# A two-layer graph network on one core: six sums per batch move from GpSimd to VectorE, two copies change engine, and the loads, writes and sums of a few batches take other steps

## The chip, the cores and the metric

The kernel runs on one core of a Trainium2 chip. The metric is the device time of one execution in microseconds. A core has TensorE (matmuls), VectorE, ScalarE, GpSimd and SyncE; the profile calls them PE, DVE, ACT, POOL and SP. Each works through its own list of instructions in order, and semaphores let one wait for another. SyncE issues almost all DMAs here, GpSimd a few.

## The reference

All arithmetic is in float32. There are 32 batches of 512 nodes with 512 features; the adjacency matrices are 512 x 512 for each batch.

```python
# layer 0
h = relu(layernorm(x))
deg = sum(adj, axis=-1)
agg = (adj @ h) / max(deg, 1e-6)
x = x + relu(concat([h, agg]) @ W0.T)
# layer 1
h = relu(layernorm(x))
q, k = split(h @ Wqk); v = h @ Wv
agg = adj @ (k * mask)
w = (q * agg).sum(-1) * mask / sqrt(512)
x = x + softmax(w, over the nodes)[:, None] * v
```

## The kernel before

The kernel rearranges the algebra so that each batch needs four groups of products: Y (transposed h times the right half of W0), O (h times the left half plus scaled adj times Y, which gives the new x), TV (the new h times a combined weight matrix and Wv), and U (adj times masked h). Every product of 512 x 512 matrices is done with seven products of half-size blocks in place of eight, in the manner of Winograd and Strassen. That needs sums and differences of the blocks of each operand beforehand and of the results afterwards. Operands live in tiles of seven slots: four slots hold the blocks, three take sums.

`left_sums` and `right_sums` (lines 102 to 115) give the four additions of a left and of a right operand, in an order in which a later one uses an earlier one. `add` and `sub` (lines 93 to 97) do them on VectorE, or on the engine given as `on`. `copy` (line 100) is a ScalarE activation. `product` (from line 118, matmuls at line 130) is a generator: it issues the matmuls of one step and yields, and between them it issues the copies of a finished PSUM tile (`pp`, `pq`) and the additions of results (`pr`, `m5`, `pq`). It uses its seven blocks in the order 1, 2, 6, 5, 7, 3, 4. A TV step (matmuls at line 467) works in the same way on four PSUM banks.

The instruction order of every engine is written by hand. `Plan.at(n, f)` puts a piece of work behind step n of the running phase, and `run` plays a phase and its plan. So the place of a line in the plan fixes where its instructions stand on every engine, with the DMAs on SP among them. An engine that waits holds up everything behind it on its own list. O and TV have 14 steps, U and Y have 7. The main loop runs O(i), TV(i-1), U(i), Y(i+1) for i from 0 to 31; batch 0 has a start of its own in `start()`.

The work beside the products comes in these classes:

- `FrontH` (batch b, first h): `load` reads x in two halves into buffers of tag `n` (two buffers), `stats` takes statistics on VectorE, `variance` and `shift` finish them (a power on GpSimd at line 248 between two VectorE instructions), `write` normalizes on ScalarE (line 258) and sends the chunk to a DRAM scratch `dhT`, `to.read` brings it back to `shT` in another order and `turn` transposes it on VectorE into `hT` (tile `wide`).
- `FrontA` (adj): `load` into the same two `n` buffers, `sum` adds a row on ScalarE (line 330), `degrees` clamps and inverts on VectorE (lines 334 and 335), `write` scales on ScalarE (line 343) and sends to `daT`; `turn` fills the tile `aT`, and `sums` calls `left_sums` on it.
- `FrontH1` (second h): statistics, `write`, `mask` (line 379), `masked_sums`, `turn`, `sums` and `inner_sums` (tile `h1T`); `keep` stores the new x as `dx`.
- `Stream` loads the seven blocks of W0's left half again in every batch (`w<-dw`, line 409), three buffers.
- `Post` (the end of a batch, during the next batch's phases): `recombine` on tile `tv`, `dot`, softmax pieces, `apply` on ScalarE (line 566), `add_x1`, a GpSimd DMA that adds the stored x (line 573, `tv<-dx`), and `store` on SP (line 589), which waits for it.

In O the plan before gives the four sums of Y and two of the four sums of adj to GpSimd:

```python
right_y = right_sums(of(Y[i]), nc.gpsimd)
p.at(1 + k // 2, FA[i].sums, k, nc.gpsimd)
```

Of the kernel before, what the change touches and what calls it, by code (L numbers as in the profile page):

```python
# [22 lines left out]
def kernel(  # L23
# [35 lines left out]
    nc = tc.nc  # L59
    B, N, F = x.shape  # L60
    C = N // P
# [37 lines left out]
    def copy(o, i):  # L99
        nc.scalar.activation(o, i, AF.Copy)  # L100

    def left_sums(s, on=None):

        return [
            lambda: add(s(4), s(2), s(3), on), lambda: sub(s(6), s(0), s(2), on),
            lambda: sub(s(5), s(4), s(0), on), lambda: sub(s(2), s(1), s(5), on),
        ]

    def right_sums(s, on=None):
        return [  # L110
            lambda: sub(s(4), s(1), s(0), on), lambda: sub(s(6), s(3), s(1), on),
            lambda: sub(s(5), s(3), s(4), on), lambda: sub(s(1), s(2), s(5), on),
        ]

    def of(t):
        return lambda i: t[:, i]
# [104 lines left out]
    X, AT_, DEG, W, Y, H1M, H1T, U, TV = ({} for _ in range(9))  # L221
# [65 lines left out]
    class FrontH:  # L287
# [23 lines left out]
        def sums(self, i):  # L311
            left_sums(of(hT))[i]()

    class FrontA:
# [33 lines left out]
                AT_[self.b] = slots("aT", 1, f"aT_{self.b}")  # L348
            self.to.turn(h, AT_[self.b])

        def sums(self, i, on=None):
            left_sums(of(AT_[self.b]), on)[i]()

    class FrontH1:

# [278 lines left out]
        for k in range(C):  # L634
            nc.tensor.transpose(p[:, ts(k, P)], src[:, ts(k, P)], identity)

    def keep_chunk(dst, c, name):
        copy(
            dst[:, 2 * (c // 2):2 * (c // 2) + 2, :, ts(c % 2, P)],
            held.pop((name, c)).rearrange("p (a b i) -> p a b i", a=2, b=2),  # L640
        )

    FH, FA, F1 = {}, {}, {}
# [25 lines left out]
    def start():  # L669
# [3 lines left out]
        fa = FA[0] = FrontA(0)  # L673
# [9 lines left out]
        fh = FH[1] = FrontH(1)  # L683
# [17 lines left out]
        h0 = hT  # L701
# [3 lines left out]
        for c in range(C):  # L705
            v = block(f"h_{c}").rearrange("p a f -> p (a f)")
            nc.scalar.activation(
                in_order(v), natural(X[0][:, c, :]), AF.Relu, scale=t[1][:, c:c + 1], bias=t[2][:, c:c + 1]
            )
            turn_chunk(v, c, "h")  # L710
            if c > 0:
                keep_chunk(h0, c - 1, "h")
        keep_chunk(h0, 3, "h")
        r2, l0 = right_sums(of(w2R)), left_sums(of(h0))
        for f in r2[:3] + l0[:3] + r2[3:] + l0[3:]:
            f()
# [12 lines left out]
        p = Plan()  # L729
# [23 lines left out]
        p = Plan()  # L753
# [47 lines left out]
        p = Plan()  # L801
# [47 lines left out]
    with tc.manual_schedule(engines=engines):  # L849
        weights, mvR = start()  # L850
        post = None
        for i in range(B):
# [4 lines left out]
            if i > 0:  # L857

                p = Plan()
                for n in range(4):  # L860
                    p.at(2 * n + 1, stream.load)
                right_y = right_sums(of(Y[i]), nc.gpsimd)
                p.at(0, right_y[0])
                p.at(0, right_y[2])
                for k in (1, 3):
                    p.at(1 + k // 2, FA[i].sums, k, nc.gpsimd)
                    p.at(1 + k // 2, right_y[k])
                if i == 1:
                    for k, g in enumerate(weights[4:]):
                        p.at(3 + 2 * k, g)  # L870
                    fa = FA[2]
                    for h in range(2):
                        for c in range(2):
                            p.at(2 + 2 * h + c, fa.sum, 2 * h + c)
                            p.at(6 + 2 * h + c, fa.write, 2 * h + c)
                        p.at(4 + 2 * h, fa.degrees, h)
                    FH[3] = FrontH(3)
                    p.at(10, FH[3].load, 0)
                    p.at(11, FH[3].load, 1)
                f1 = F1[i - 1]  # L880
                for k in range(4):
                    p.at(k // 2, f1.sums, k)
                if post is not None:
                    for c in range(C):
                        p.at(2 + c, post.apply, c)
                    p.at(3, post.add_x1, 0)
                    p.at(5, post.add_x1, 1)
                    p.at(9, post.store, 0)
                    p.at(11, post.store, 1)
                for k in range(4):  # L890
                    p.at(2 + k, f1.inner_sums, k, 0, 7)
                if 1 < i and i + 2 < B:
                    fh = FH[i + 2]
                    for c in range(C):
                        p.at(3 + c, fh.stats, c)
                        p.at(10 + c, fh.write, c)
                    p.at(7, variance, fh.t)
                    p.at(9, shift, fh.t)
                if more:
                    th = FH[i + 1]  # L900
                    p.at(2, th.to.read, 1)
                    p.at(11, th.turn, 0)
                if 1 < i and i + 2 < B:
                    fa = FA[i + 2] = FrontA(i + 2)
                    p.at(12, fa.load, 0)
                p.at(12, f.stats, 0)
                p.at(12, f.stats, 1)
                p.at(13, variance, f.t, 0, 2)
                run(layer0_out(i, stream.take), 14, p)


                post = Post(i - 1, F1[i - 1])
                p = Plan()
                p.at(0, f.stats, 2)
                p.at(0, shift, f.t, 0, 2)
                p.at(0, f.stats, 3)
                p.at(1, variance, f.t, 2, 4)
                if last:
                    p.at(1, FA[i].factor)
                p.at(3, shift, f.t, 2, 4)  # L920
                for c in range(C):
                    p.at([2, 3, 5, 6][c], f.write, c)
                    p.at(8 + c, f.mask, c)
                p.at(1, f.keep)
                for k in range(4):
                    p.at([10, 12, 12, 12][k], f.masked_sums, k)
                if 1 < i and i + 2 < B:
                    p.at(1, fa.load, 1)
                    for h in range(2):
                        for c in range(2):  # L930
                            p.at(4 + 2 * h + c, fa.sum, 2 * h + c)
                        p.at(7 + 2 * h, fa.degrees, h)
                if i == 1:
                    fa = FA[3] = FrontA(3)
                    p.at(11, fa.load, 0)
                    p.at(13, fa.load, 1)
                    fh = FH[3]
                    for c in range(C):
                        p.at(4 + c, fh.stats, c)
                        p.at(9 + c, fh.write, c)  # L940
                    p.at(7, variance, fh.t)
                    p[9].insert(0, lambda t=fh.t: shift(t))
                if more:
                    p.at(3, th.turn, 1)
                    for k in range(4):
                        p.at(5 + k // 2, th.sums, k)
                p.at(8, f.to.read, 0)
                p.at(9, f.to.read, 1)
                for k in range(7):
                    p.at(12 + k // 4, post.recombine, k, 0, 0)  # L950
                run(layer1_tv(i - 1), 14, p)


            p = Plan()
# [7 lines left out]
            if i == 0:  # L962
                fh = FH[2]
# [35 lines left out]
            if more:  # L999
                p = Plan()  # L1000
                fb = FA[i + 1]
                p.at(2, fb.turn, 0)
                p.at(3, fb.turn, 1)
                p.at(4, fb.sums, 0)
                p.at(4, fb.sums, 2)
                p.at(1, load_x, i + 1)
                if i + 2 < B:
                    p.at(5, FH[i + 2].to.read, 0)
                if i > 0:
                    p.at(0, post.shift)  # L1010
                    p.at(1, post.exponents)
                    p.at(2, post.row_sum)
                    p.at(4, post.weights)
                    for k in range(7):
                        p.at(3 + k // 2, post.recombine, k, None, 1)
                p.at(2, FA[i].factor)
                if i == 0:
                    for c in range(C):
                        p.at(c, fh.write, c)
                    for k in range(1, 4):  # L1020
                        p.at(3 + k, weights[k])
                    FA[2] = FrontA(2)
                    p.at(3, FA[2].load, 0)
                    p.at(6, FA[2].load, 1)
                elif i == 1:
                    p.at(0, fa.degrees, 1)
                    for c in range(C):
                        p.at(2 + c, fa.write, c)
                    FH[4] = FrontH(4)
                    p.at(5, FH[4].load, 0)  # L1030
                    p.at(6, FH[4].load, 1)
                elif i + 3 < B:
                    p.at(0, FH[i + 3].load, 1)
                run(layer0_y(i + 1), 7, p)

        final = Post(B - 1, F1[B - 1])
        p = Plan()
# [71 lines left out]
```

## Time and profile before

| | |
|---|---|
| median of 4 runs | 2297.28 us (2296.23 to 2299.43) |
| the profiled execution's own time | 2296.23 us |
| its span in the profile | 2294.1 us |
| PE busy | 2248.9 us (98%) |
| DVE busy | 1968.2 us (86%) |
| ACT busy | 1027.9 us (45%) |
| POOL busy | 508.6 us (22%) |
| DMA moved | 463.65 MB, 202 GB/s |

The busy time of an engine is the sum over its instructions in one profiled execution; register, branch, semaphore and DMA-issuing instructions are not counted. The own time holds about 2 us outside the span. The profile names a group of instructions by line, engine, operation and tiles (`out<-in`, buffer numbers left out); a wait is named by the waiting instruction and by what released it. The phases of the middle batches follow each other evenly: O takes 24.2 us, TV 21.15, U and Y 12.1 each.

### The profile page before, as it was taken

What the parts mean: (1) busy time and instruction counts of PE and PEld (TensorE: products, weight loads), DVE (VectorE), ACT (ScalarE), POOL (GpSimd) and SP (SyncE); (2) the same over time, 40 slices, a digit from 0 to 9 for tenths busy, and PEclk for the clock granted to TensorE, in tenths of its full rate; (3) what the DMA queues carried; (4) which work ended last, traced back from release to release, by engine and by line L of the source; (5) the groups of instructions that cost most, each with busy time, mean ns of one, the idle gap of its engine ahead of it and who ended that gap; (6) DMA issues with size and microseconds to landing.
All of it is one profiled execution on the core that took longest, in us unless ns stands there. A gap on an engine that the chain in (4) does not pass through costs nothing.

```text
span 2294.1 us, 32535 instructions
## 1 busy us (share of the span) xinstructions
PE 2248.9 (98%) x10372; PEld 1968.5 (86%) x10372; DVE 1968.2 (86%) x3619; ACT 1027.9 (45%) x1903; POOL 508.6 (22%) x453
## 2 busy tenths in 40 slices
PE   7999999999999999999999999999999999999996
PEld 6788888888888888888888888888888888888885
DVE  6798898888898888898888988888988889888878
ACT  4454434444444544344454344443444543444332
POOL 0202222112222112222022221122220222211222
PEclk9999999999999999999999999999999999999998
DMA  9978877877778877777877778877778787787552
GB/s 220 226 202 229 214 195 194 223 216 210 207 191 205 226 218 205 207 183 211 229 215 207 194 185 228 218 201 202 193 205 226 215 207 199 191 219 213 152 139 64
DMA packets 409594, 463.65 MB, mean 202 GB/s; under 512 B 37680, under 2 KB 271152, under 8 KB 405328
## 3 DMA queue, kind: packets, MB, share of 16 engines
q1 hardware_dynamic: 400176, 428.56, 69.1%
q0 software_dynamic: 8928, 32.51, 8.0%
q8 instruction: 82, 1.34, 0.3%
q14 instruction: 88, 0.72, 0.1%
q10 hardware_dynamic: 320, 0.52, 0.1%
HBM read 293.93 MB, written 167.51 MB: 201 GB/s over the span
## 4 chain that ended last, share of the span: by engine, by line
PE 82%; DVE 8%; DMA 5%; SPq 2%; issue 1%; POOL 1%; ACT 1%; DVEq 0%; ACTq 0%; POOLq 0%
PE ptv L467 23%; PE pp_o L130 16%; PE pp_y L130 9%; PE pp_u L130 8%; PE pq_o L130 8%; PE pq_y L130 4%; PE pq_u L130 4%; PE pr_o L130 4%; PE pr_y L130 2%; PE pr_u L130 2%; DVE tv L94 2%; DMA dhT<-n 2%; DMA tv<-dx 1%; DMA a<-in_adj_dram 1%; SPq L204 1%
## 5 line engine op out<-in xcount | busy, mean ns | idle before, releaser
L467 PE MATMUL ptv<-mv,h1T 128*128 128x256 f32 x3136 | 684.3, 379 | 6.2 <-ACT m_tv L100 4.8
L467 PEld LDWEIGHTS ptv<-mv,h1T 128*128 128x128 f32 x3136 | 595.0, 190 | 90.3 <-ACT m_tv L100 7.6
L94 DVE TENSOR_TENSOR tv<-tv 128x256 f32<-128x256 f32 (+1 forms) x644 | 322.0, 512 | 11.6
L97 DVE TENSOR_TENSOR h1T<-h1T 128x512 f32<-128x512 f32 (+2 forms) x195 | 277.7, 1437 | 1.2
L100 ACT ACTIVATE tv<-ptv 128x512 f32<-128x512 f32 (+1 forms) x372 | 188.0, 540 | 151.0 <-PE ptv L467 144.8
L130 PE MATMUL pp_y<-wide 128*128 128x256 f32 x1024 | 243.5, 381 | 2.5 <-ACT y L100 2.5
L130 PE MATMUL pp_o<-y,aT 128*128 128x256 f32 x1024 | 241.9, 379 | 0.0
L130 PE MATMUL pp_u<-h1m,aT 128*128 128x256 f32 x1024 | 241.9, 379 | 0.0
L130 PE MATMUL pp_o<-w,wide 128*128 128x256 f32 x992 | 234.4, 379 | 0.5 <-ACT o L100 0.5
L130 PEld LDWEIGHTS pp_y<-wide 128*128 128x128 f32 x1024 | 195.5, 191 | 29.6 <-ACT y L100 2.9
L97 POOL TENSOR_TENSOR y<-y 128x512 f32<-128x512 f32 x124 | 216.2, 1743 | 15.5 <-DVE y L94 12.9
L130 PEld LDWEIGHTS pp_u<-h1m,aT 128*128 128x128 f32 x1024 | 194.6, 190 | 26.9 <-issue 0.5
L130 PEld LDWEIGHTS pp_o<-y,aT 128*128 128x128 f32 x1024 | 194.5, 190 | 26.4
L548 POOL PARTITION_ALL_REDUCE gtop<-top x32 | 12.5, 391 | 903.4 <-DVE top L545 885.5
L130 PEld LDWEIGHTS pp_o<-w,wide 128*128 128x128 f32 x992 | 188.4, 190 | 26.5 <-ACT o L100 0.9
L100 ACT ACTIVATE o<-pp_o 128x512 f32<-128x512 f32 x96 | 57.3, 597 | 298.3 <-PE pp_o L130 298.3
L100 ACT ACTIVATE y<-pp_y 128x512 f32<-128x512 f32 x128 | 76.4, 597 | 239.1 <-PE pp_y L130 234.1
L248 POOL TENSOR_TENSOR rstd<-rstd,mhalf 128x2 f32<-128x2 f32 (+1 forms) x96 | 78.4, 817 | 446.2 <-DVE rstd L247 446.2
L100 ACT ACTIVATE xu<-pp_u 128x512 f32<-128x512 f32 x128 | 76.4, 597 | 198.0 <-PE pp_u L130 198.0
L94 DVE TENSOR_TENSOR tv<-ptv,m_tv 128x512 f32<-128x512 f32 (+1 forms) x124 | 73.1, 622 | 103.3 <-ACT m_tv L100 89.8
L94 DVE TENSOR_TENSOR tv<-ptv,tv 128x512 f32<-128x512 f32 x248 | 141.7, 613 | 13.9 <-PE ptv L467 11.2
L330 ACT ACTIVATE a<-a 128x512 f32<-128x512 f32 x128 | 80.2, 627 | 110.1 <-DMA a<-in_adj_dram 110.1
(113 smaller groups left out, 3465.7 us busy)
## 6 DMA issues: line engine op xcount, KB each, us to landing
w<-dw SPq DMA_DIRECT2D x217, 256.0 KB, 3.2
xu<-in_x_dram SPq DMA_DIRECT2D x128, 256.0 KB, 5.3
a<-in_adj_dram SPq DMA_DIRECT2D x256, 128.0 KB, 3.1
dh1T<-h1m SPq DMA_DIRECT2D x128, 256.0 KB, 3.3
dx<-xu SPq DMA_DIRECT2D x32, 1024.0 KB, 5.0
sh1T<-dh1T SPq DMA_DIRECT2D x256, 128.0 KB, 3.3
shT<-dhT SPq DMA_DIRECT2D x248, 128.0 KB, 4.7
daT<-a SPq DMA_DIRECT2D x124, 256.0 KB, 3.0
```

Of the source, the lines that this page charges most:

```text
L94: (on or nc.vector).tensor_tensor(o, a, b, op=ALU.add)
L97: (on or nc.vector).tensor_tensor(o, a, b, op=ALU.subtract)
L100: nc.scalar.activation(o, i, AF.Copy)
L130: nc.tensor.matmul(p[:, rc, :], lt[:, LEFT[k], dk, ts(rc, P)], right[:, dk, :], start=first and n == 0, stop=True, skip_group_check=True,)
L204: nc.sync.dma_start(out=t[q * R:(q + 1) * R, :, :], in_=rows[:, 2 * h:2 * h + 2, :])
L248: nc.gpsimd.tensor_tensor(rstd[:, a:b], rstd[:, a:b], mhalf[:, a:b], op=ALU.pow)
L330: nc.scalar.activation(v, v, AF.Copy, accum_out=DEG[self.b][:, c:c + 1])
L467: nc.tensor.matmul(banks[n][:, :, ts(i, P)], left[:, LEFT[k], LEFT_IN[j], :], mvR[:, RIGHT[k], RIGHT[j], :, :], start=first and i == 0, st ...
L548: nc.gpsimd.partition_all_reduce(self.gtop, self.top, channels=P, reduce_op=ReduceOp.max)
```

## The change

Seven edits, in three phases of the main loop and in the start:

1. The four sums of Y in O go to VectorE, and so do the two sums of adj; sums 1 and 3 of both stand at steps 2 and 4, where they stood at 1 and 2. `FrontA.sums` loses its engine argument.
2. In the start, the four normalizations of batch 0's h and their transposes are issued first, and then the four copies out of PSUM; the first two of these copies go to VectorE.
3. Y of batch 1: the four writes of h of batch 2 stand at steps 2, 3, 4 and 4 (before: 0 to 3), and the first load of adj of batch 2 at step 5 (before: 3). On SP the four x loads of batch 1 now stand ahead of these writes, and the reads `shT` ahead of both adj loads.
4. O of batch 1: the writes of adj of batch 2 stand at steps 8 to 11 (before: 6 to 9), the degrees at 5 and 7 (before: 4 and 6).
5. O of batch 1: the loads of x of batch 3 stand at steps 12 and 13 (before: 10 and 11).
6. TV from batch 2 of the loop on: the sums over adj stand at steps 4, 6, 8 and 10 (before: 4 to 7).
7. There, too, the degrees stand at 8 and 12 (before: 7 and 9).

```diff
-        def sums(self, i, on=None):
-            left_sums(of(AT_[self.b]), on)[i]()
+        def sums(self, i):
+            left_sums(of(AT_[self.b]))[i]()
...
-    def keep_chunk(dst, c, name):
-        copy(
+    def keep_chunk(dst, c, name, by=copy):
+        by(
...
             turn_chunk(v, c, "h")
-            if c > 0:
-                keep_chunk(h0, c - 1, "h")
-        keep_chunk(h0, 3, "h")
+        for c in range(C):
+            keep_chunk(h0, c, "h", nc.vector.tensor_copy if c < 2 else copy)
...
-                right_y = right_sums(of(Y[i]), nc.gpsimd)
+                right_y = right_sums(of(Y[i]))
                 p.at(0, right_y[0])
                 p.at(0, right_y[2])
                 for k in (1, 3):
-                    p.at(1 + k // 2, FA[i].sums, k, nc.gpsimd)
-                    p.at(1 + k // 2, right_y[k])
+                    p.at(2 + 2 * (k // 2), FA[i].sums, k)
+                    p.at(2 + 2 * (k // 2), right_y[k])
...
                             p.at(2 + 2 * h + c, fa.sum, 2 * h + c)
-                            p.at(6 + 2 * h + c, fa.write, 2 * h + c)
-                        p.at(4 + 2 * h, fa.degrees, h)
+                            p.at(8 + 2 * h + c, fa.write, 2 * h + c)
+                        p.at(5 + 2 * h, fa.degrees, h)
                     FH[3] = FrontH(3)
-                    p.at(10, FH[3].load, 0)
-                    p.at(11, FH[3].load, 1)
+                    p.at(12, FH[3].load, 0)
+                    p.at(13, FH[3].load, 1)
...
-                            p.at(4 + 2 * h + c, fa.sum, 2 * h + c)
-                        p.at(7 + 2 * h, fa.degrees, h)
+                            p.at(4 + 4 * h + 2 * c, fa.sum, 2 * h + c)
+                        p.at(8 + 4 * h, fa.degrees, h)
...
                     for c in range(C):
-                        p.at(c, fh.write, c)
+                        p.at([2, 3, 4, 4][c], fh.write, c)
...
                     FA[2] = FrontA(2)
-                    p.at(3, FA[2].load, 0)
+                    p.at(5, FA[2].load, 0)
                     p.at(6, FA[2].load, 1)
```

## The prediction

> **What bounds the kernel now.** I read the page first, then TensorE's own waits, then the timelines of one batch in the middle, and last the places where TensorE stands still.
>
> ```profile
> span 2294.1 us, 32535 instructions
> PE 2248.9 (98%) x10372; PEld 1968.5 (86%) x10372; DVE 1968.2 (86%) x3619; ACT 1027.9 (45%) x1903; POOL 508.6 (22%) x453
> ```
>
> TensorE is the bound: 2248.9 of 2294.1 us. In the batch from 449.78 to 519.28 it never stops, so a batch costs 69.5 us whatever the others do. A change of order and engine can only win what TensorE waits, and lose by making it wait. Its waits (total us, times, longest):
>
> ```profile
> PE h L635 <- ACT h L707: 14.1, 2, 13.6
> PE ptv L467 <- ACT m_tv L100: 4.8, 6, 2.0
> PE pp_y L130 <- ACT y L100: 2.5, 1, 2.5
> PE pq_o L130 <- DMA w<-dw: 1.5, 1, 1.5
> PE ptv L467 <- DVE h1T L97: 1.2, 1, 1.2
> PE pp_o L130 <- ACT o L100: 0.5, 1, 0.5
> ```
>
> Outside the first 13.6 us, about 11 us can be had. The timelines of O in that middle batch show how VectorE and GpSimd stand there (start, us, engine, line):
>
> ```profile
> 451.79 1.75 DVE L94 TENSOR_TENSOR h1T<-h1T 128x512 f32<-128x512 f32 x1
> 453.47 5.12 DVE L97 TENSOR_TENSOR h1T<-h1T 128x512 f32<-128x512 f32 x3
> 458.62 2.04 DVE L94 TENSOR_TENSOR h1T<-h1T 128x896 f32<-128x896 f32 x1
> 460.58 2.15 DVE L97 TENSOR_TENSOR h1T<-h1T 128x896 f32<-128x896 f32 x1
> 464.78 1.08 DVE L97 TENSOR_TENSOR h1T<-h1T 128x896 f32<-128x896 f32 x1
> ...
> 476.46 0.68 DVE L442 SCALAR_TENSOR_TENSOR xu<-pp_o,xu 128x512 f32<-128x512 f32 x1
> 451.44 3.23 POOL L97 TENSOR_TENSOR y<-y 128x512 f32<-128x512 f32 x2 [0.21 <-DVE y L94]
> 461.73 1.97 POOL L573 DMA_DIRECT2D tv<-dx  x2
> ```
>
> While GpSimd does the six sums (451.44 to 461.7) a 128x896 add takes VectorE 2.04 to 2.15 us, and 1.08 once they are over. A 128x512 add takes 1.71 there, 0.69 elsewhere (the aT and wide groups). Only after its sums can GpSimd issue tv<-dx, and the output stores on SP wait for that (243.6 us in SP's waits). The costliest of the six m_tv waits, in the batch from about 1565:
>
> ```profile
> 1587.92 2.20 SPq L589 DMA_DIRECT2D out_dram<-tv  x4
> 1594.88 1.74 SPq L204 DMA_DIRECT2D a<-in_adj_dram  x4
> 1599.03 0.63 ACT L330 ACTIVATE a<-a 128x512 f32<-128x512 f32 x1 [5.01 <-DMA a<-in_adj_dram]
> 1604.78 0.63 ACT L330 ACTIVATE a<-a 128x512 f32<-128x512 f32 x1 [1.29 <-DMA a<-in_adj_dram]
> 1605.41 1.06 ACT L100 ACTIVATE m_tv<-ptv 128x512 f32<-128x512 f32 x2
> 1606.04 6.31 PE L467 MATMUL ptv<-mv,h1T 128*128 128x256 f32 x28 [1.97 <-ACT m_tv L100]
> ```
>
> Late store, late write of h behind it, late load of adj into the same buffers, ScalarE stuck on a sum over adj with the m_tv copies queued behind: TensorE loses 1.97 us. The wait in Y of batch 1 has the same form:
>
> ```profile
> 88.71 0.16 DVE L252 SCALAR_TENSOR_TENSOR nmr<-mv,rstd 128x4 f32<-128x4 f32 x1 [0.62 <-POOL rstd L248]
> 88.91 0.81 ACT L258 ACTIVATE n<-n,nmr,rstd 128x512 f32<-128x512 f32 x1 [4.00 <-DVE nmr L252]
> 89.63 0.58 ACT L100 ACTIVATE y<-pp_y 128x512 f32<-128x512 f32 x1
> 90.26 1.99 PE L130 MATMUL pp_y<-wide 128*128 128x256 f32 x8 [2.53 <-ACT y L100]
> ```
>
> **Part 1, sums of Y and adj on VectorE (31 batches).** Added to VectorE: 186 adds of 128x512 at 0.69 us, 128 us, or 0.605 start to start, 3.6 us a batch. Given back: 96 h1T adds at 1.373 instead of 0.69 (66 us), 93 at 1.545 and 31 at 2.048 instead of 1.08 (43 and 30), 32 at 0.920 (7): 146 us. VectorE's busy time falls by some 18 us, to about 1950. Its order in O, from 451.8: two sums of y to 453.1, four h1T adds to 455.5, aT and y to 456.7, two 896 adds to 458.7, statistics to 459.5, o and xu to 460.8, aT and y to 462.0, then as before. TensorE's steps begin every 1.727 us from 449.78. It needs y's slot 5 at step 5 (458.4; ready 453.1), slots 6 at step 9 (465.3; 456.7), aT's slot 2 at step 11 (468.8; 461.4), y's slot 1 at step 13 (472.2; 462.0). Nothing is within 5 us, so the sums cost the path nothing, under TensorE's 24.2 us of O; uncovered, they would be 3.6 us a batch. VectorE reaches shift (470.66 today) about 2.5 us sooner. GpSimd issues tv<-dx when ScalarE's apply is done, near 455.4 and 456.6 instead of 461.7. Its landing took 5.6 to 8.9 us, so the stores at steps 9 and 11 find it done; the writes of h and the eight loads of adj behind them on SP come 2.5 us sooner, and by up to 5 in the bad batches.
>
> A rule against this: the Trainium skill, "SBUF — State Buffer", under "SBUF: two separate sides", says that VectorE can lock GpSimd out of their shared port so that it can't write the descriptors of its own DMAs, and gives 3100 ns for a DMA of 620. VectorE's adds would now stand around tv<-dx. The row: issued at 461.73 beside a two-input add of VectorE, it took 1.97 us for two; over all 62, 0.87 to 1.20 each. By the row it moves 5 us forward; by the rule each loses 2.5 and both moves are eaten, and the adj loads stay late (case B). I take the row, since the same kind of add was beside it.
>
> **Part 2, sums over adj at every second step of TV.** The adds stay at four of 0.63 + 0.19 us; on ScalarE the third and fourth now stand behind the m_tv copies, with a mask between. Behind a late load wait only masks, which VectorE's h1m adds and U need at the end of TV; in my count the masks end 17.2 us into TV, against 19.1 in the middle batch. The second half of adj (used at 487.6, 13.6 into TV) has about 3 us in hand. VectorE's second degrees come after the h1m adds, and the writes of adj in U find them. Of the m_tv waits (0.40, 0.81, 0.20, 0.93, 1.97, 0.45: 4.76) a late first half could leave some; bounds 3.0 and 4.76, and as parts 1 and 2 both help, I take 4.3.
>
> **Part 3, h of batch 2 written later in Y of batch 1.** The copy of y now precedes the first write, so the 2.53 us go. Next on ScalarE is the second y copy, behind one write: 88.9 + 0.7, then ready at 90.2, needed at 91.0. Slack 0.8 us, so the next wait is not far. On SP the four x loads come forward, the four dhT writes stay, and the four shT reads go ahead of the eight adj loads: issue at about 96 and 98, against 97.7 and 102.3. The w load behind them lands near 104.5, needed at 106.8. Bounds 1.7 to 2.53, take 2.5.
>
> **Part 4, adj of batch 2 written later in O.** The copies m_o and o now precede the writes that wait for VectorE's degrees: the 0.48 us go. VectorE starts y's sums near 98.9 and ends the last mv add near 118.6 (122.4 today); TensorE needs it at 121.5. L442 frees a PSUM bank near 125.0, needed at 125.9. The x loads of batch 3 (eight DMAs) stay behind the four daT writes; they land near 124 and 127, before their statistics. Take 0.5.
>
> **Part 5, the first copies.** ScalarE's four normalizations run without copies between, so the transposes wait neither the 0.53 us at 16.09 nor the 0.1 before 17.27. VectorE pays two PSUM copies, not in the trace as such; its adds out of PSUM take 0.68, and it sits idle 2.08 us at 19.05: nothing. But TensorE runs here at half pace (eight matmuls of pp_y in 3.42 us from 18.18, then 0.216 each from 21.4; the page's PEclk row is too coarse to show it). By the row alone, full pace came 5.3 us after the gapless start at 16.09; that start moves to 13.59, worth 1.5 us. The Trainium skill, "TensorE: Matmul & The Clock Gate", "What's actually happening", has windows of 3.4 us that run free of the program: either the same window (0.3 us, half the gap) or the one before (2.0). I take 1.2, range 0.3 to 2.0. All that follows up to batch 1 is paced by TensorE (through its pm products at 65.3) and moves along.
>
> Left: the w wait at 181.4 (adj, then x loads ahead of it on SP) and h1T at 2254, whose cover does not change: 0.
>
> **Sum.** 1.2 + 2.5 + 0.5 + 4.3 = 8.5 us off the profiled execution's 2296.23 (span 2294.1): 2287.7. That run was the fastest of four; the median is 1.05 higher, so 2288.8.
>
> **Rivals.** B: tv<-dx is held up, or VectorE's lead is lost in waits for statistics, and the m_tv waits stay: 4.2 us, 2293.1. For: the port rule; against: part 2 alone takes two sums out of the way. D: the early waits only move to the next place (0.8 us of slack in Y, 0.9 at L442, the w loads): 4.3 to 5 us, 2292.8. For: an ordering this tight at 70 us; against: everything there was counted.
> C, slower: VectorE becomes the bound in O. If the long h1T adds do not shrink, 3.6 us come on top. L442 ends at 477.14 and frees a bank that the second product of TV needs at 478.7 to 479.1. From about 1.8 us of added VectorE time TensorE waits every batch: (3.6 - 1.8) x 31 = 56 us, 2353. Against it: the same add takes 1.08 at 464.78 and 2.15 at 460.58, in one batch.
>
> **How the numbers follow.** Two kernels closer than 0.2% (4.6 us) can't be told apart. Forecast 0.68 (2285 to 2291.5), B 0.15, D 0.10, C 0.07. B and D lie on the border of 2292.7: half of them count as faster. Faster 0.68 + 0.12 = 0.80, same 0.13, slower 0.07. The range runs from 2285.0 (all waits gone, early clock) to 2294.5, over B and D.
>
> **What would show it.** Right: 128x512 h1T adds near 0.69 us and 896 near 1.08, VectorE near 1950 us; tv<-dx issued before the seventh step of O; no wait on y near 88, none on m_tv; TensorE still at 69.5 us a batch. Wrong: a wait on VectorE at L467 in every batch (C), tv<-dx taking 3 us on GpSimd (B), a new wait at 90 to 130 (D).

## The result and the profile after

The changed kernel takes 2292.44 us (median of 31 runs, 2289.2 to 2297.14), the kernel before beside it 2296.62 us (51 runs). The ratio is 0.9982, 95% interval 0.9977 to 0.9987: 4.2 us less. A second comparison gave 0.9990 (0.9983 to 0.9996). Both intervals stay below 1, and the gain is under the 0.2% that the prediction called measurable. The prediction said 8.5 us and 2288.8. The time lies outside the band given to the forecast itself (2285 to 2291.5) and inside the full range of 2285.0 to 2294.5, which was drawn over rivals B and D as well. About half of the forecast gain is missing, and the profile shows a new loss at one place.

The page of the changed kernel, its own time 2293.06 us:

```profile
span 2291.0 us, 32519 instructions
PE 2248.0 (98%) x10372; PEld 1970.3 (86%) x10372; DVE 1931.1 (84%) x3807; ACT 1027.8 (45%) x1901; POOL 183.8 (8%) x267
```

VectorE has taken on 186 additions and yet is busy for 37 us less; GpSimd keeps a third of its time. TensorE's waits (total us, times, longest):

```profile
PE h L635 <- ACT h L707: 13.5, 1, 13.5
PE pq_o L130 <- DMA w<-dw: 7.6, 1, 7.6
PE ptv L467 <- DVE h1T L97: 1.2, 1, 1.2
PE ptv L467 <- DVE xu L94: 0.2, 1, 0.2
```

The waits on y, o and m_tv are gone, all the waits that the sum counted on. The wait for w has grown from 1.5 to 7.6 us. TensorE's timeline there, in O of batch 2 (start, duration, and in brackets the idle time before and what ended it):

```profile
172.62 1.89 PE L130 MATMUL pp_o<-y,aT 128*128 128x256 f32 x8
182.12 3.75 PE L130 MATMUL pq_o<-w,wide 128*128 128x256 f32 x8 [7.61 <-DMA w<-dw]
185.66 2.15 PE L130 MATMUL pq_o<-y,aT 128*128 128x256 f32 x8
187.65 1.89 PE L130 MATMUL pp_o<-w,wide 128*128 128x256 f32 x8
```

The same wait in the kernel before:

```profile
181.41 1.97 PE L130 MATMUL pq_o<-w,wide 128*128 128x256 f32 x8 [1.47 <-DMA w<-dw]
```

After the wait of 7.61 us the next eight matmuls take 3.75 us where eight take 1.89, and the eight after those 2.15: TensorE comes back at half clock, about half its full pace. The granted clock shows it, 0.74 and 0.58 of full speed in two windows of 5 us (the columns: busy time of PE, PEld, DVE, ACT and POOL, then granted PEclk, DMA share, GB/s). After:

```profile
177.00:182.00 5.00, 0.00 (x0) 0.00 (x0) 4.93 (x8) 0.00 (x0) 0.00 (x0) 0.74 1.04 214
182.00:187.00 5.00, 4.88 (x13) 4.00 (x14) 3.77 (x9) 0.00 (x0) 0.94 (x1) 0.58 0.96 203
```

Before:

```profile
177.00:182.00 5.00, 3.53 (x17) 2.82 (x16) 4.93 (x4) 0.60 (x1) 5.00 (x4) 1.00 0.98 223
```

The DMA engines are near full load in both kernels (share 1.04 and 0.98), so the share alone does not explain the late w. What differs is which transfers are in flight beside it, and this stands in the timelines of SP and GpSimd. After:

```profile
167.89 5.37 SPq L204 DMA_DIRECT2D n<-in_x_dram  x8
173.36 0.37 SPq L409 DMA_DIRECT2D w<-dw  x1
171.95 2.10 POOL L573 DMA_DIRECT2D tv<-dx  x2 [3.54 <-ACT tv L566]
```

Before:

```profile
171.52 5.37 SPq L204 DMA_DIRECT2D n<-in_x_dram  x8
176.99 0.37 SPq L409 DMA_DIRECT2D w<-dw  x1
184.24 2.09 POOL L573 DMA_DIRECT2D tv<-dx  x2
```

The w load is issued 3.6 us earlier than before, but lands 8.6 us after its issue. The two accumulating stores tv<-dx of batch 0, 512 KB each, are issued 12.3 us earlier, mostly because GpSimd has no sums ahead of them (9.3 us in e3_sums_alone below), and now stand 1.4 us ahead of w. The DMA view of 160 to 192 us (issues, KB each, median us to landing), after:

```profile
tv<-dx POOLq DMA_DIRECT2D x2, 512.0 KB, 8.7
w<-dw SPq DMA_DIRECT2D x4, 256.0 KB, 8.4
```

and before:

```profile
w<-dw SPq DMA_DIRECT2D x4, 256.0 KB, 4.6
tv<-dx POOLq DMA_DIRECT2D x2, 512.0 KB, 7.2
```

Three numbers account for the two profiles. "Arrival" is when TensorE is free for the `pq_o` product that waits for w (start of the product before it, plus 1.73); "next block" is the start of pp_o after the two pq_o products; "rest" is the span less that.

| profile | arrival | w wait | next block | rest | span |
|---|---|---|---|---|---|
| before | 179.78 | 1.47 | 184.94 | 2109.2 | 2294.1 |
| changed | 174.35 | 7.61 | 187.65 | 2103.4 | 2291.0 |

TensorE arrives 5.4 us earlier; from arrival to the next block it takes 13.3 us instead of 5.2 (6.1 more of waiting, 2.0 at half clock); the rest, free of m_tv waits, is 5.8 us shorter. 5.4 - 8.1 + 5.8 = 3.1 us, the difference of the two spans.

### The profile page after: what moved, and what is told of

It is laid out like the page before. It is cut to its first block, busy times and chain, and to the rows that moved or that the text cites. A ratio compares the mean times of both kernels' runs of the same rounds, so it can differ in the third digit from the quotient of the medians.

```text
span 2291.0 us, 32519 instructions
## 1 busy us (share of the span) xinstructions
PE 2248.0 (98%) x10372; PEld 1970.3 (86%) x10372; DVE 1931.1 (84%) x3807; ACT 1027.8 (45%) x1901; POOL 183.8 (8%) x267
## 4 chain that ended last, share of the span: by engine, by line
PE 95%; DVE 2%; DMA 1%; issue 0%; SPq 0%; POOL 0%; ACT 0%; DVEq 0%
PE ptv L467 28%; PE pp_o L130 19%; PE pq_o L130 10%; PE pp_y L130 9%; PE pp_u L130 9%; PE pq_u L130 5%; PE pq_y L130 5%; PE pr_o L130 5%; PE pr_u L130 2%; PE pr_y L130 2%; DVE wide L94 1%; PE pm L805 1%; DMA xu<-in_x_dram 1%; DMA w<-dw 0%; DVE tv L94 0%; DMA saT<-daT 0%
## 5 line engine op out<-in xcount | busy, mean ns | idle before, releaser
L97 DVE TENSOR_TENSOR h1T<-h1T 128x512 f32<-128x512 f32 (+2 forms) x195 | 168.2, 877 | 1.3
L130 PE MATMUL pq_o<-w,wide 128*128 128x256 f32 x496 | 119.3, 384 | 7.6 <-DMA w<-dw 7.6
L130 PE MATMUL pq_o<-y,aT 128*128 128x256 f32 x512 | 121.2, 380 | 0.0
L130 PE MATMUL pq_y<-wide 128*128 128x256 f32 x512 | 121.0, 379 | 0.0
```

The costliest lines, as they stand in the source:

```text
L97: (on or nc.vector).tensor_tensor(o, a, b, op=ALU.subtract)
L130: nc.tensor.matmul(p[:, rc, :], lt[:, LEFT[k], dk, ts(rc, P)], right[:, dk, :], start=first and n == 0, stop=True, skip_group_check=True,)
```

## The experiments

The parts are numbered as in the prediction: 1 the sums of Y and adj in O, 2 the sums over adj in TV, 3 Y of batch 1, 4 O of batch 1, 5 the first copies. The theory was that w is late because tv<-dx meets it in a stretch in which the DMA engines are full; the rivals were the order on SP's queue, and TensorE's earlier arrival. Each kernel ran beside the kernel before on the same chip, and ratios are to that; medians of different groups are not compared (the kernel before had 2295.72, 2293.33 and 2294.59 us in the three).

**e1_dx_later: the stores moved behind the w load.**

```diff
-                    p.at(3, post.add_x1, 0)
-                    p.at(5, post.add_x1, 1)
+                    p.at(8 if i == 2 else 3, post.add_x1, 0)
+                    p.at(8 if i == 2 else 5, post.add_x1, 1)
```

> The changed kernel, in which the two accumulating stores of batch 0's corrections (tv<-dx, 512 KB each) are issued at step 8 of O(2) instead of steps 3 and 5, behind GpSimd's variance work: after about 186 us instead of at 172. Theory (the w load of O(2) came late because it shares a stretch that the DMA engines already fill with the two stores): w lands about 4.4 us after its issue as in the kernel before, the wait of pq_o for w falls from 7.6 us to about 3.3 us, the stretch at half clock behind it is short or gone, and the time is 2286 to 2288 us (changed kernel: 2292.4). Rival (the place of the w load behind the eight loads of n on SP's queue is all that counts, the stores are innocent): the wait stays at 7.6 us and the time at 2292.4 us.

Ratio 0.9975 (0.9967 to 0.9983), 2290.16 us. TensorE's waits, its timeline, and two lines of ScalarE's in the following TV:

```profile
PE ptv L467 <- ACT tv L100: 3.3, 2, 2.1
PE pq_o L130 <- DMA w<-dw: 1.1, 1, 1.1
```

```profile
175.89 1.97 PE L130 MATMUL pq_o<-w,wide 128*128 128x256 f32 x8 [1.09 <-DMA w<-dw]
198.10 5.45 PE L467 MATMUL ptv<-mv,h1T 128*128 128x256 f32 x24 [1.25 <-ACT tv L100]
205.61 11.02 PE L467 MATMUL ptv<-mv,h1T 128*128 128x256 f32 x42 [2.06 <-ACT tv L100]
197.45 1.36 ACT L100 ACTIVATE tv<-ptv 128x512 f32<-128x512 f32 x3 [6.01 <-DMA out_dram<-tv]
204.35 0.63 ACT L330 ACTIVATE a<-a 128x512 f32<-128x512 f32 x1 [4.14 <-DMA a<-in_adj_dram]
```

TensorE arrives at 174.65, as early as in the changed kernel, and SP's order is unchanged, yet the w wait is 1.1 us and nothing runs at half clock behind it: both rivals fall. That is lower than the 3.3 us that I expected, so the earlier arrival alone costs nothing. The time fell less than expected because the next TV now waits, 3.3 us in all. The stores, issued at 186.45, keep `tv` occupied until the output has left it, and ScalarE's copies wait for that (first wait, 1.25 us). In the second wait, 2.06 us, the copies stand behind a sum over adj that waits for a late load of adj. After it 42 matmuls take 11.02 us where 9.1 would do.

**e2_w_first: the eight n loads behind the w load.**

```diff
+                if i == 2:
+                    FH[4] = FrontH(4)
+                    p.at(1, FH[4].load, 0)
+                    p.at(1, FH[4].load, 1)
...
-                    FH[4] = FrontH(4)
-                    p.at(5, FH[4].load, 0)
-                    p.at(6, FH[4].load, 1)
```

> The changed kernel, in which the eight loads of n that stand ahead of the late w load on SP's queue (x of the next batch, from steps 5 and 6 of Y(1)) are issued in step 1 of O(2), behind that w load. Theory (order on the queue plus a full stretch of DMA): w is issued at about 168 us, ahead of the stores of tv<-dx at 172, and lands before TensorE wants it at 182: wait 0 to 1 us, no half clock, 2284 to 2285 us. Rival (the DMA engines are behind by so much that something must come late whatever the order): the wait moves to a later w load or to the statistics of n, 2290 to 2292 us.

Ratio 0.9994 (0.9986 to 1.0002), 2293.64 us, no better than the changed kernel. Its SP and GpSimd timelines, and TensorE's:

```profile
166.81 0.34 SPq L409 DMA_DIRECT2D w<-dw  x1
173.83 3.67 SPq L409 DMA_DIRECT2D w<-dw  x3
171.52 2.09 POOL L573 DMA_DIRECT2D tv<-dx  x2 [2.94 <-ACT tv L566]
```

```profile
175.25 1.89 PE L130 MATMUL pq_o<-w,wide 128*128 128x256 f32 x8
184.01 3.75 PE L130 MATMUL pp_o<-w,wide 128*128 128x256 f32 x8 [5.14 <-DMA w<-dw]
```

The first w load is there in time, and the next, issued 2.3 us after the stores, comes late in its place. The rival was right: the order only chooses which transfer suffers.

**e3_sums_alone: part 1 on the kernel before.** The edit to the kernel before:

```diff
-                right_y = right_sums(of(Y[i]), nc.gpsimd)
+                right_y = right_sums(of(Y[i]))
...
-                    p.at(1 + k // 2, FA[i].sums, k, nc.gpsimd)
-                    p.at(1 + k // 2, right_y[k])
+                    p.at(2 + 2 * (k // 2), FA[i].sums, k)
+                    p.at(2 + 2 * (k // 2), right_y[k])
```

> The kernel before with one part of the change alone: the sums of Y and adj in O on VectorE, at every second step, instead of on GpSimd. Theory (the sums leave GpSimd, so tv<-dx is issued some 12 us earlier and meets the w load): the m_tv waits of the stages behind are gone (-4 us), the y and o waits of the start stay (3.0 us), the w wait rises from 1.5 to 5 or 6 us: 2296.5 us within 1, the time of the kernel before. Rival (this part is pure gain, and the w load comes late for the earlier TensorE alone): 2292.3 us.

Ratio 1.0001 (0.9992 to 1.0009), 2294.95 us; in microseconds a little below the expectation, like the kernel before on this chip.

```profile
PE pq_o L130 <- DMA w<-dw: 7.0, 2, 6.6
PE pp_y L130 <- ACT y L100: 2.8, 1, 2.8
```

The theory held: in the profile no m_tv wait, and a w wait of 6.55 us at 185.27 with half clock behind it. Here TensorE arrives at 178.56, 1.2 us earlier than before (179.78), w is issued 0.5 us earlier, and still it waits: the stores are enough.

**e4_sums_on_gpsimd: the change without part 1.** The edit to the changed kernel (`FrontA.sums` has its engine argument back):

```diff
-                right_y = right_sums(of(Y[i]))
+                right_y = right_sums(of(Y[i]), nc.gpsimd)
...
-                    p.at(2 + 2 * (k // 2), FA[i].sums, k)
-                    p.at(2 + 2 * (k // 2), right_y[k])
+                    p.at(1 + k // 2, FA[i].sums, k, nc.gpsimd)
+                    p.at(1 + k // 2, right_y[k])
```

> The changed kernel with the sums of Y and adj in O back on GpSimd at the old steps; all other parts of the change stay. Theory: the gains of the start stay (start 1.7, y 2.5, o 0.5 us), part of the m_tv waits stays, tv<-dx is issued at about 184 us as in the kernel before and doesn't meet the w load, whose wait is about 3.3 us because TensorE arrives earlier: about 2290 us. Rival (the m_tv waits come from these sums alone, so all of them stay): 2293.5 us.

Ratio 0.9971 (0.9960 to 0.9983), 2288.51 us, a little better than expected.

```profile
PE pp_o L130 <- ACT o L100: 1.7, 1, 1.7
PE ptv L467 <- DVE xu L442: 1.3, 2, 0.7
PE pq_o L130 <- DMA w<-dw: 0.3, 1, 0.3
```

The w wait is 0.3 us, tv<-dx is issued at 183.57, and there is no m_tv wait, so the rival falls. VectorE's 128x896 additions are long again (1444 ns), and its busy time is 1983.7 us: 53 us more than in the changed kernel, with small waits in the first three batches (o 1.7, xu 1.3, m_o 1.2, m_u 0.3 us). On balance the edit that the change is named after earns nothing here: without it these waits stand in the profile, with it the 7.6 us for w.

**e5_first_copies: part 5 on the kernel before.** The edit to the kernel before (`keep_chunk` takes the engine as in the change):

```diff
-            if c > 0:
-                keep_chunk(h0, c - 1, "h")
-        keep_chunk(h0, 3, "h")
+        for c in range(C):
+            keep_chunk(h0, c, "h", nc.vector.tensor_copy if c < 2 else copy)
```

> The kernel before with part 5 alone: the first transposed chunks of h are copied after all four normalizations, two of the copies on VectorE. Theory: the first transposes run without the gap of 0.53 us, full clock comes earlier (pp_y's third product of step 6 at 21.4 instead of 23.2 us), and all up to O of batch 1 moves along by the same 1.7 us, since TensorE paces it; the y wait near 88 stays at 2.5 to 2.8 us. 2295.0 us against 2296.6 of the kernel before. Rival: the y wait is paced by the x loads and ScalarE's writes, not by TensorE, so it swallows the gain (4.2 us there): 2296.6 us.

Ratio 0.9999 (0.9991 to 1.0007), 2292.65 us. TensorE's timeline:

```profile
20.50 1.89 PE L130 MATMUL pp_y<-wide 128*128 128x256 f32 x8
89.27 3.46 PE L130 MATMUL pp_y<-wide 128*128 128x256 f32 x8 [3.17 <-ACT y L100]
```

The third product of the first Y starts 2.7 us earlier than in the first profile of the kernel before (20.50 against 23.16), and the lead is lost by 89: the write of h at 87.92 (before: 88.91) follows its loads and statistics, so TensorE arrives earlier and waits longer, and this time half clock followed. The rival was right. Alone, part 5 brings nothing that was measured; part 3, which puts the copy of y ahead of that write, is what lets a lead through.

**e6_no_dx_batch0: the stores left out.**

```diff
-                    p.at(3, post.add_x1, 0)
-                    p.at(5, post.add_x1, 1)
+                    if i > 2:
+                        p.at(3, post.add_x1, 0)
+                        p.at(5, post.add_x1, 1)
```

> The changed kernel without batch 0's two accumulating stores of corrections (tv<-dx): the output of batch 0 lacks its residual x1. It measures what these two stores cost in place. Theory (the two transfers and the w load share a full stretch of DMA, and in e1_dx_later the stores only came too late for the tv buffers): w wait 1.1 us as in e1_dx_later, no half clock, no wait on tv in the next TV: 2285.5 to 2287 us (changed kernel 2292.4, e1_dx_later 2290.2). Rival (the transfers ahead of w are the backlog by themselves, or the tv waits of e1_dx_later come from something else): w wait over 4 us or tv waits of 3 us stay, 2290 us or more.

Ratio 0.9963 (0.9949 to 0.9976), 2284.87 us, a little below the expectation. The kernel leaves the residual out of batch 0's output; it serves to measure only. The w wait is 1.7 us and no wait on tv is left:

```profile
PE pq_o L130 <- DMA w<-dw: 1.7, 1, 1.7
PE ptv L467 <- DVE h1T L97: 1.2, 1, 1.2
```

With TensorE's arrival the same to a hundredth (174.35), the next block starts at 179.74 instead of 187.65: the two stores, where the change puts them, cost 7.9 us in the profile.

**e7_sums_mixed: sums on GpSimd in O of batch 2 alone.**

```diff
-                right_y = right_sums(of(Y[i]))
+                on = nc.gpsimd if i == 2 else None
+                right_y = right_sums(of(Y[i]), on)
...
-                    p.at(2 + 2 * (k // 2), FA[i].sums, k)
-                    p.at(2 + 2 * (k // 2), right_y[k])
+                    at = 1 + k // 2 if i == 2 else 2 + 2 * (k // 2)
+                    p.at(at, FA[i].sums, k, on)
+                    p.at(at, right_y[k])
```

> The changed kernel with the sums of Y and adj on GpSimd at the old steps in O of batch 2 alone, on VectorE in all others. It should put the issue of batch 0's tv<-dx near 181 us, between 172 (changed kernel) and 186 (e1_dx_later). Theory (these two stores must neither meet the w load before 176 nor end after TV's first eviction at about 190): w wait 1.1 us, tv wait 0 to 0.6, xu wait 0.7: 2286 to 2287.5 us. Rival (there is no gap: the stretch is so full that the stores must delay something): 2289 to 2291 us.

Ratio 0.9972 (0.9962 to 0.9982), 2287.05 us.

```profile
176.12 1.97 PE L130 MATMUL pq_o<-w,wide 128*128 128x256 f32 x8 [0.76 <-DMA w<-dw]
179.78 2.09 POOL L573 DMA_DIRECT2D tv<-dx  x2
```

There is a gap, as the theory had it: stores issued at 179.8 disturb neither w nor the copies into `tv`. The profile shows 0.76 us for w here, and nothing for tv; the next block starts at 179.64. The ratio alone does not set it apart from e1_dx_later or the changed kernel; the last group does.

**e8_mixed_w_first: both.** The edits of e7_sums_mixed and e2_w_first.

> e7_sums_mixed with the eight loads of n behind the w load on SP's queue as in e2_w_first. Theory: with tv<-dx out of the way the order on the queue does help: w wait 0, about 1 us better than e7_sums_mixed, 2285 to 2286.5 us. Rival (as in e2_w_first the wait moves to the next w load, now behind the n loads): no better than e7_sums_mixed.

Ratio 0.9970 (0.9959 to 0.9981), 2286.83 us: the same as e7_sums_mixed.

```profile
PE pp_o L130 <- DMA w<-dw: 1.9, 1, 1.9
PE pq_o L130 <- DMA w<-dw: 1.0, 1, 1.0
```

My theory fell: tv<-dx is issued at 178.71 here, 4.9 us behind the w load of the next block (173.81), and still that load is late. What is left just ahead of it on SP's queue is the eight n loads and four reads of shT; that they delay it was not tried apart.

**c1_before_again, c2_after_again, c3_mixed_again, e9_adj_sums_alone: one group on one chip.** The first three are the kernel before, the changed kernel and e7_sums_mixed without further edits; the last is part 2 on the kernel before:

```diff
-                            p.at(4 + 2 * h + c, fa.sum, 2 * h + c)
-                        p.at(7 + 2 * h, fa.degrees, h)
+                            p.at(4 + 4 * h + 2 * c, fa.sum, 2 * h + c)
+                        p.at(8 + 4 * h, fa.degrees, h)
```

> The kernel before, profiled a second time beside the others. Theory: its m_tv waits are no fixed 4.8 us, because they hang on when loads of adj land (part 5 alone, the same program after the start, showed 1.4 us in two): they come out anywhere from 1 to 5 us, the y wait at 2.5 to 2.8, the w wait at 0.2 to 1.5. Rival: they are a property of the program's order and come out at 4.8 us in six again. Ratio 1 within 0.1%.

> The changed kernel, profiled a second time beside the others, as the measure for e7_sums_mixed on the same chip. Theory: the w wait in O of batch 2 with its stretch at half clock comes back (5 to 8 us of wait), since its cause lies in the order of the issues: ratio 0.9977 to 0.9987. Rival: it was chance of that one execution; then the wait is 1 to 3 us and the ratio 0.9965.

> e7_sums_mixed once more (sums on GpSimd in O of batch 2 alone), beside the changed kernel. Theory: about 6 us of w wait and 1.9 us of half clock less than the changed kernel, some of it already in its fastest executions: ratio to the kernel before 0.997, 3 us or more below the changed kernel. Rival: the difference between the two so far (0.9972 and 0.9982) was the chip's: no difference.

> The kernel before with part 2 alone: in TV the sums over adj at every second step, the degrees at steps 8 and 12. Theory (part 2 suffices for the m_tv waits, as e4_sums_on_gpsimd had none): no m_tv wait, the y wait stays at 2.5 to 2.8 us and the w wait at 0.2 to 1.5: ratio 0.998 to 0.9995. Rival (only the earlier issue of tv<-dx or the shift of batch 2 takes them away): m_tv waits of 1.4 to 4.8 us as in the kernel before, ratio 1.

| kernel | median us | ratio | arrival | w wait | next block | rest |
|---|---|---|---|---|---|---|
| c1_before_again | 2295.31 | 1.0003 (0.9995 to 1.0011) | 183.07 | 1.58 | 188.44 | 2107.0 |
| c2_after_again | 2292.65 | 0.9990 (0.9983 to 0.9996) | 174.54 | 5.29 | 185.02 | 2103.2 |
| c3_mixed_again | 2285.91 | 0.9959 (0.9946 to 0.9973) | 175.63 | 0.35 | 179.77 | 2105.0 |
| e9_adj_sums_alone | 2291.01 | 0.9984 (0.9977 to 0.9990) | 183.16 | 1.16 | 188.11 | 2103.0 |

The late w came back in c2_after_again, 5.29 us with half clock for eight matmuls; the ratio lies just above the expected 0.9977 to 0.9987. c3_mixed_again (5 executions) is 6.7 us below it, and the intervals do not touch: this version beats both kernels. The kernel before, profiled again, waits differently, for y and for w longer than expected:

```profile
PE pp_y L130 <- ACT y L100: 3.8, 1, 3.8
PE ptv L467 <- ACT m_tv L100: 2.9, 4, 1.3
PE pq_o L130 <- DMA w<-dw: 1.6, 1, 1.6
PE pp_o L130 <- POOL y L97: 1.0, 1, 1.0
```

So m_tv was 4.8, 2.9 and, in e5_first_copies, 1.4 us in executions of which only the start differs: its size is no property of the program's order. e9_adj_sums_alone has no m_tv wait:

```profile
PE pp_y L130 <- ACT y L100: 2.7, 1, 2.7
PE pq_o L130 <- DMA w<-dw: 1.2, 1, 1.2
PE pp_o L130 <- POOL y L97: 1.0, 1, 1.0
```

Part 2 alone brings about 3.6 us (2291.01 against the kernel before's 2294.59 in this group). The whole change brought 1.9 us here and 4.2 in the first comparison, so part 2 is worth about as much as all of it: by the medians, what parts 3 to 5 win is spent at the w load.

## Why the prediction was half right

- **The step that failed** is the line "Left: the w wait at 181.4 (adj, then x loads ahead of it on SP) ... whose cover does not change: 0". It measured 6.1 us more wait and 2.0 us lost at half clock, 8.1 in place of 0. I had dated the new issue of tv<-dx in a middle batch (5 to 6 us earlier) and asked only what comes free behind it. In O of batch 2 it moves 12.3 us, to 1.4 us ahead of the w load, in a stretch whose DMA share is about 1. e1_dx_later, e6_no_dx_batch0 and e7_sums_mixed, with TensorE as early, wait 0.8 to 1.7 us there; e3_sums_alone, with TensorE 1.2 us earlier, waits 6.6. The cause is the meeting of tv<-dx and w; by what means the one slows the other was not separated. With the stores out of the way the gain is near the forecast: 8.5 us in e6_no_dx_batch0, 6.3 in e7_sums_mixed, 8.7 in c3_mixed_again.
- **Rival D** (chance 0.10) named "the w loads" among the places to which waits could move, but looked for the new wait at 90 to 130 us; it came at 174. Its reason was an ordering that is too tight, and the runs show the stores of another queue. That its 2292.8 us lies so near the measured 2292.44 is luck: D counted 4.3 to 5 us won, while the two profiles show 11.2 won and 8.1 lost.
- **Parts 3, 4 and 5**: 4.2 us were counted, 5.4 measured between the first two profiles. The third product at the start comes at 21.41 instead of 23.16, 1.75 us against the 1.2 taken; the start of O of batch 1 moves from 99.00 to 94.44, so part 3 gives 2.8 against 2.5; and TV of batch 0 from 124.06 to 118.66, so part 4 gives 0.8 against 0.5. In the second pair TensorE arrives 8.5 us earlier, since the kernel before then waited 3.8 us for y, ran at half clock behind it, and waited 1.0 us for a sum of y on GpSimd; the first profile was mild in these. For the start it was not: the third product comes at 20.96 in c1_before_again and at 21.51 in c2_after_again, so there part 5 wins nothing. Over all profiles it comes at 20.96 to 23.57 with the old start (four) and at 20.38 to 21.51 with the new one (ten). Part 5's size is therefore not shown by one pair.
- **m_tv waits**: 4.3 us counted. The rest of the span, in which they lay, is 5.8 us shorter in the first pair and 3.8 in the second; the waits themselves were 4.8 and 2.9 us, and the about 1 us on top was not traced. In one profile each, either part is enough, part 1 (e3_sums_alone) or part 2 (e9_adj_sums_alone). The prediction left open which.
- **Part 1 on VectorE**: 128x896 additions 1077 ns, 128x512 near 0.69 us, and no wait of TensorE on VectorE in O, as forecast. In the middle batch tv<-dx is issued 5.8 us into O (before: 12.0), and the batch still takes 69.50 us. VectorE falls by 37 us against the 18 forecast. Two terms were off: the 96 instructions xu<-o of line 442 also fell, from 821 to 692 ns, 12 us that were not counted; and additions in a row start 0.605 us apart though each lasts 0.69, so that the sum of 128 us counted overlaps, some 16 us over 186 by my estimate. The two together are more than is missing; the balance was not traced. Rival C did not come, and e4_sums_on_gpsimd shows that even the longer VectorE time stays hidden in the middle batches.
- **Rival B**, the port: two tv<-dx took GpSimd 2.10 us between VectorE's additions in the changed kernel and 2.09 before; over all 62 one took 0.97 us in the median, before 1.12. No lock-out is seen. Nor does the page that the prediction cites, "SBUF — State Buffer", "SBUF: two separate sides", state one for this case: its 3100 ns belong to a VectorE copy, and further down the same section says that additions did not stall the DMA. So rival B had little ground. What takes longer is the landing, in the median of all 62 7.9 us after the issue against 6.8; why was not tried.

What stays open: each profile is one execution, and the profiled execution of c2_after_again (2290.27 us) is faster than its median by 2.4 us. How large the w wait is in a typical execution was not measured. How the stores slow the w load is open too: the share of the DMA engines was near 1 before as well. Nor was it tried why e4_sums_on_gpsimd, e5_first_copies and c3_mixed_again wait 0.8 to 1.2 us for m_o near 49 us.

## What to carry to other kernels

When an engine that issues DMAs loses work, its DMAs move too: date their new issue in the first and last batches as well as in a middle one, and list which transfers with a deadline they now meet. A gain ahead of a full DMA stretch can be paid back in it, and reordering one queue only picked the transfer that is late here; the stores needed a slot between w and the reuse of `tv`, and six additions left on GpSimd in a single batch gave it. Profile the kernel before twice before putting a size on waits of a microsecond: here the same waits came to 4.8, 2.9 and 1.4 us.

## What was not expected of the hardware

A pause of TensorE can cost more than its length, and the length does not decide alone. Behind the start, all pauses of 3.17 us and more in these profiles (3.17, 3.79, 5.14, 5.29, 6.55 and 7.61) were followed by half clock, about 3.5 to 3.8 us for the next eight matmuls. After shorter ones it went both ways: 2.53 us in the kernel before and 2.84 in e3_sums_alone were followed by eight in 1.99, but 2.69 us in e9_adj_sums_alone by eight in 3.51:

```profile
90.83 3.51 PE L130 MATMUL pp_y<-wide 128*128 128x256 f32 x8 [2.69 <-ACT y L100]
```

and in e1_dx_later a pause of 2.06 us, 7.5 us after one of 1.25, was followed by a granted clock of 0.66:

```profile
205.00:210.00 5.00, 4.39 (x13) 3.54 (x14) 1.01 (x4) 5.00 (x13) 0.00 (x0) 0.66 0.84 280
```

The Trainium skill, "TensorE: Matmul & The Clock Gate", "What's actually happening", puts the return to half clock behind an idle window of about 3.4 us, and says that the windows run free of the program. That pauses of 2.5 to 2.8 us were punished in one execution and not in another is in keeping with free windows, though no run shows the windows themselves. That 2.1 us (with 1.25 shortly before) and 2.7 us were punished does not agree with a whole idle window of 3.4, and the measurement decides.
